# A graph-attention kernel in which the first turn waits for the one-hot: two banks of z, two banks of sums

## The chip, the cores and the metric

The kernel runs on one core of a Trainium2 chip. The metric is the device time of one execution in microseconds; the time of a version is the median over its runs.

## What is computed

One block of a graph network over 12,500 nodes with 128 features and 400,000 edges, which are sorted by their destination. After two norms of the nodes, a GATv2 attention with 8 heads of 16 features, a residual, a norm, and a two-layer GELU network follow:

```python
x_l = (x @ W_l).reshape(n, H, C)
x_r = (x @ W_r).reshape(n, H, C)
e = (ea @ W_e).reshape(-1, H, C)
m = jax.nn.leaky_relu(x_l[src] + x_r[dst] + e, NEG_SLOPE)
alpha = jnp.einsum('ehc,hc->eh', m, att)
amax = jax.ops.segment_max(alpha, dst, num_segments=n)
expa = jnp.exp(alpha - amax[dst])
denom = jax.ops.segment_sum(expa, dst, num_segments=n)
a = expa / (denom[dst] + 1e-16)
out = jax.ops.segment_sum(x_l[src] * a[:, :, None], dst, num_segments=n)
```

`loop` edges from each node to itself are part of it; the kernel deals with them where it finishes a group of nodes.

## The kernel before

A first part (about 190 us) norms the nodes and forms x_l and x_r. From then on the main loop goes through the edges in 782 **pairs** of 512 edges each. It is a software pipeline, one pair per **round**, and the order of its instructions is written out by hand: a table `stages` gives for each step the round in which it handles pair c, and in a round the steps are issued in the order of the table. A step of pair c in the steady part:

- `gather` (POOL, L1033): four indirect DMAs, 128 rows of x_l each, into a slot of a ring of 30 slots. The gathers of c reuse the slot of c-30 and wait until its sums are done.
- `place` (DVE, L1100, round c-1): the one-hot of the destinations, 96 rows of `ea`. The other 32 rows are the edges' attributes, loaded by DMA.
- `combine` (TensorE, round c): four transposes of the gathered rows into a bank of PSUM, the **turns** (L1127), and on top of them the **closing product** (L1132) of x_r's window and the edge weights with `ea`. The result is z = x_l[src] + x_r[dst] + e. Three banks of z take turns.
- `slope` (ACT, L1150, round c+1): zs = 0.2 z. `bend` (DVE, L1164, round c+1): m = max(z, zs).
- `score` (TensorE, L1185, round c+2, one round later for the first pair of a batch): the attention scores, 64 rows for a batch of eight pairs.
- Once per batch of eight pairs: scans for the lowest score of each segment (DVE, L1193 to L1214), the exponential (`weigh`, ACT, L1218), its transpose (`turn`, TensorE, L1225) and a copy of it beside the rows (`keep_turned`, ACT, L1235).
- `times` (DVE, L1246, round c+12): the gathered rows times their weights, in place in the ring.
- `own_nodes` (DVE, L1259, once per four pairs): the one-hot `own` of the destinations within a node window of 32, from `local` numbers that ACT copies into PSUM (L1295).
- `collect` (TensorE, L1277, round c+13): four products of `own` with the ring's rows, 32x144, the **sums** of the pair.
- `keep_sums` (ACT, L1289, round c+14): the copy `rec` of the sums out of PSUM, and L1308 the DMA that stores it.

In a round's order `keep_sums` and `put` stand first, then `collect`, `times`, `slope`, `combine`, `score`, `place`, `bend`. So in one round ACT begins with rec of c-1 and TensorE with sums of c. The work on finished groups of nodes (lines 1376 to 1632; names `f_...`, `acc`) and late parts of the first stage (lines 697 to 767; names `l_...`, `aux`) is woven into the rounds on fixed places.

PSUM has eight banks: before the change three of z, one of the scores, one of the turned weights `t`, one of the sums (three places of 144 columns, and two places of `local` beside them), `acc` and `aux`. Waits between engines are found by bank and by buffer: an instruction that writes or reads a bank waits for the last user of that bank on another engine. An engine waits by a semaphore that the other engine raises; `declare_no_dep` takes out a wait that another one covers, with its reason in the text.

Of the kernel before, what the change touches and what calls it, by code (L numbers as in the profile page):

```python
# [13 lines left out]
F32 = mybir.dt.float32  # L14
# [8 lines left out]
P = 128  # L23
# [14 lines left out]
QP = 4  # L38
# [10 lines left out]
W = 32  # L49
# [5 lines left out]
SX = P + 2 * H  # L55
# [876 lines left out]
def window_edges(  # L932
# [9 lines left out]
    nc = tc.nc  # L942
    SP = mybir.EngineType.SP
    KP = UP * KU
    EPR = UP * U
# [7 lines left out]
    pairs = [{} for _ in range(n_pr)]  # L953
    batches = []
    while not batches or batches[-1][-1] + 1 < n_pr:
        c = batches[-1][-1] + 1 if batches else 0
# [22 lines left out]
    with ExitStack() as es:  # L979
        once = es.enter_context(tc.tile_pool(name="e_once", bufs=1))  # L980
        load = es.enter_context(tc.tile_pool(name="e_load", bufs=2))
        work = es.enter_context(tc.tile_pool(name="e_work", bufs=3))
        ps1 = es.enter_context(tc.tile_pool(name="e_ps1", bufs=1, space=PSUM))
# [10 lines left out]
        ring = once.tile([P, RING, KP, SX], F32, name="ring")  # L994
# [102 lines left out]
        def place(c):  # L1097

            d = pairs[c]
            placed = nc.vector.tensor_scalar(  # L1100
                d["ea"][0:WN].rearrange("p (a b) -> p a b", b=OW),
                d["dl"][0:WN].rearrange("p (a b) -> p a b", b=OS)[:, :, 0:OW],
                wid[0:WN], None, op0=OP.is_equal,
            )
            if c % QP == 0:
                for ins in d["loads"]:
                    tc.add_manual_dep(
                        placed.ins, ins.name,
                        mybir.DependencyInfo(mybir.DependencyClass.Sync, mybir.DependencyReason.DATA),
                        reason="TensorE reads what was loaded beside the one-hot, and waits for VectorE alone",  # L1110
                    )

        scored = {}
        z_banks = [ps1.tile([P, EPR], F32, name=f"z{i}") for i in range(3)]
        z_used = []

        def z_bank():

            z_used.append(1)
            return z_banks[len(z_used) % 3]  # L1120

        def combine(c):

            d, e = pairs[c], sum(edges_of(c))
            z = z_bank()
            d["turns"] = [
                nc.tensor.matmul(  # L1127
                    z[:, j * P : (j + 1) * P], row_of(c, j)[:, 0:P], ident, start=(j == 0), stop=False, is_transpose=True
                ).ins
                for j in range(e // P)  # L1130
            ]
            d["closed"] = nc.tensor.matmul(z[:, :e], d["zw"], d["ea"][:, :e], start=False, stop=True).ins  # L1132
            d["z"] = z
            for ins in d["loads"]:
                tc.declare_no_dep(
                    d["closed"], ins, reason="VectorE waited for it ahead of the one-hot, which is read here too"
                )
            scored[c] = {i for i, p in enumerate(pairs[max(0, c - 9) : c], max(0, c - 9)) if "score" in p}
# [3 lines left out]
            for ins in pairs[c]["turns"]:  # L1142
                tc.declare_no_dep(reader.ins, ins, reason="TensorE made it ahead of the product that closes z")

        slopes = [work.tile([P, EPR], F32, name=f"zs{i}", bufs=1) for i in range(3)]

        def slope(c):
            d, e = pairs[c], sum(edges_of(c))
            d["zs"] = slopes[c % 3]
            sloped = nc.scalar.activation(d["zs"][:, :e], d["z"][:, :e], AF.Copy, scale=SLOPE)  # L1150
            only_last(sloped, c)
            if c >= 3:
                for ins in (pairs[c - 3]["bent"], pairs[c - 3]["sloped"]):
                    tc.declare_no_dep(
                        sloped.ins, ins, reason="TensorE waited for it ahead of z, which is read here"
                    )
            d["sloped"] = sloped.ins
# [105 lines left out]
                op=OP.is_equal,  # L1263
            )

        PLACES = 3
        sum_bank = ps1.tile([P, EPR], F32, name="sums")
        sum_at = [sum_bank[0:W, i * SX : (i + 1) * SX] for i in range(PLACES)]
        first = PLACES * SX
        local_at = [sum_bank[:, i : i + QP * KP] for i in (first, first + QP * KP)]  # L1270

        def collect(c):

# [11 lines left out]

        def keep_sums(c):
            d = pairs[c]
            d["rec"] = work.tile([W, SX], F32, name="rec", bufs=5)
            nc.scalar.copy(d["rec"], sum_at[c % PLACES])  # L1289
            if c >= n_pr - HASTE:  # L1290
                put(c)
            q, at = divmod(c + 2, QP)
            if at == 0 and q < len(fours):
                of_four[q]["local"] = local_at[q % 2]
                nc.scalar.copy(of_four[q]["local"], local_sb[:, q * QP * KP : (q + 1) * QP * KP])  # L1295
# [30 lines left out]
        sums = [None] * NL  # L1326
# [26 lines left out]
        def near_end(d):  # L1353
            return any(d is g for g in groups[-2:])
# [9 lines left out]
            return d[name][:, 0 : d["n"]]  # L1364

        def bank_of(d, name, ring="acc"):
            if near_end(d) and ring == "acc":
                ring = "z"
            d[name] = z_bank() if ring == "z" else ps1.tile([P, EPR], F32, name=ring)
            return d[name]  # L1370
# [425 lines left out]
        with tc.manual_schedule():  # L1796
            for r in range(-AHEAD, max(last_round, groups[-1]["round"] + 19)):
# [12 lines left out]
                for late, f in sum_stages:  # L1810
                    i, off = divmod(r - late, SUM_STEP)
# [10 lines left out]
                for late, f in late_stages:  # L1822
                    c = r - late
# [3 lines left out]
                if off == 0 and CLEARED <= t + CLEARED < NT and t >= 0:  # L1827
                    tc.declare_no_dep(
                        clear(t + CLEARED).ins, group="states",
                        reason="states stored so far lie below the tile, which the check of destinations asks",  # L1830
# [358 lines left out]
```

## Time and profile before

| what | value |
|---|---|
| median of 3 runs | 4851.8 us (4845.96 to 4852.41) |
| profiled execution | 4798.29 us |
| its span | 4796.5 us |
| mean granted TensorE clock | 0.875 |
| gathers, first to last start | 189.9 to 4660.0 us |
| DMA traffic | 536.78 MB, 112 GB/s over the span |

The profile is of one execution. A busy time is that of the engine's own instructions; "idle before" is the time in which an engine stood still ahead of an instruction, put down to what ended it. "issue" there means that the trace shows nothing that was waited for, and "remote" a word from an engine or queue that the trace does not name. PE is TensorE's matmuls and PEld its weight loads, which run beside them.

### The profile page before, as it was taken

What the parts mean: (1) busy time and instruction counts of PE and PEld (TensorE: products, weight loads), DVE (VectorE), ACT (ScalarE), POOL (GpSimd) and SP (SyncE); (2) the same over time, 40 slices, a digit from 0 to 9 for tenths busy, and PEclk for the clock granted to TensorE, in tenths of its full rate; (3) what the DMA queues carried; (4) which work ended last, traced back from release to release, by engine and by line L of the source; (5) the groups of instructions that cost most, each with busy time, mean ns of one, the idle gap of its engine ahead of it and who ended that gap; (6) DMA issues with size and microseconds to landing.
All of it is one profiled execution on the core that took longest, in us unless ns stands there. A gap on an engine that the chain in (4) does not pass through costs nothing.

```text
span 4796.5 us, 48948 instructions
## 1 busy us (share of the span) xinstructions
PE 3544.8 (74%) x14951; PEld 1790.8 (37%) x14952; DVE 2622.4 (55%) x4977; ACT 1502.6 (31%) x3825; POOL 2952.7 (62%) x3136
## 2 busy tenths in 40 slices
PE   3327777777777777777777877777778777777787
PEld 2203333333333333343333433333434333333344
DVE  5316555655655555556555555555555555555455
ACT  5302323322322323323333333333333333333222
POOL 6655666665666666666666666666666666666650
PEclk8658888888888989899898989898989898889898
DMA  6525555555543443444434334343344433434331
GB/s 185 164 75 151 141 145 144 148 146 147 142 132 93 112 110 102 104 112 105 106 93 106 100 98 102 98 101 101 91 99 108 100 100 98 102 86 103 100 96 31
DMA packets 425616, 536.78 MB, mean 112 GB/s; under 512 B 97241, under 2 KB 307210, under 8 KB 424794
## 3 DMA queue, kind: packets, MB, share of 16 engines
q1 hardware_dynamic: 282360, 266.19, 21.5%
q0 software_dynamic: 100000, 205.00, 16.5%
q10 hardware_dynamic: 42984, 62.37, 4.4%
q8 instruction: 121, 1.98, 0.2%
q14 instruction: 151, 1.24, 0.1%
HBM read 471.82 MB, written 61.42 MB: 111 GB/s over the span
## 4 chain that ended last, share of the span: by engine, by line
PE 38%; DVE 20%; another core or an unknown queue 15%; issue 12%; ACT 5%; DMA 2%; POOL 1%; ACTq 1%; SPq 0%; DVEq 0%; POOLq 0%
PE sums L1277 12%; PE z L1132 9%; PE s L1185 7%; PE z L1127 6%; DVE ea L1100 3%; DVE ring L1246 3%; DVE m L1164 3%; DVE s L1193 2%; DVE p L1207 2%; POOL ring L1033 1%; DVE p L1200 1%; ACT zs L1150 1%; ACT rec L1289 1%; PE acc L1612 1%
## 5 line engine op out<-in xcount | busy, mean ns | idle before, releaser
L1033 POOL DMA_INDIRECT ring<-xl_dram,idx_sb x3009 | 2839.8, 944 | 1637.4 <-issue 785.4
L1277 PE MATMUL sums<-ring,own 128*32 128x144 f32 x6250 | 1044.9, 317 | 979.2 <-ACT rec L1289 645.2
L1277 PEld LDWEIGHTS sums<-ring,own 128*32 128x32 f32 x6250 | 681.8, 119 | 1551.7 <-ACT rec L1289 801.2
L1164 DVE TENSOR_TENSOR m<-z,zs 128x512 f32<-128x512 f32 x782 | 532.8, 681 | 900.7 <-issue 538.8
L1132 PE MATMUL z<-ea,zw 128*128 128x512 f32 x1564 | 920.2, 674 | 10.9 <-issue 7.4
L1185 PE MATMUL s<-m,zneg 128*64 128x512 f32 x1564 | 851.2, 636 | 90.9 <-issue 71.4
L1150 ACT ACTIVATE zs<-z 128x512 f32<-128x512 f32 x782 | 464.8, 594 | 1171.5 <-PE z L1132 303.7
L1246 DVE TENSOR_TENSOR ring<-ring,t 128x512 f32<-128x512 f32 x782 | 527.8, 676 | 391.8 <-PE t L1225 179.4
L1127 PE MATMUL z<-ident,ring 128*128 128x128 f32 x3125 | 594.1, 320 | 25.2 <-DMA raw_dram<-raw 11.5
L1100 DVE TENSOR_SCALAR ea<-dl,wid 96x516 f32<-96x516 bf16 x782 | 577.7, 739 | 15.1 <-DMA zw<-xr_dram 15.1
L1289 ACT COPY rec<-sums 32x144 f32<-32x144 f32 x782 | 204.8, 262 | 1103.7 <-remote 332.0
L1127 PEld LDWEIGHTS z<-ident,ring 128*128 128x128 f32 x3125 | 379.8, 158 | 243.0 <-issue 218.1
L1185 PEld LDWEIGHTS s<-m,zneg 128*64 128x64 f32 x1564 | 165.7, 142 | 758.2 <-issue 635.0
L1193 DVE TENSOR_TENSOR_SCAN s<-g,s 64x512 f32<-64x512 bf16 x98 | 120.4, 1228 | 332.0 <-remote 100.6
L1132 PEld LDWEIGHTS z<-ea,zw 128*128 128x128 f32 x1564 | 279.3, 223 | 11.9 <-issue 8.0
L1259 DVE TENSOR_TENSOR own<-nodes,sums 128x512 f32<-128x512 f32 x195 | 132.6, 680 | 246.3 <-remote 190.0
L1218 ACT ACTIVATE p<-p 64x512 f32<-64x512 f32 x98 | 61.7, 630 | 330.0 <-DVE p L1207 128.8
L1235 ACT COPY ring<-t 128x256 f32<-128x256 f32 (+3 forms) x236 | 65.7, 344 | 253.7 <-DVE ring L1246 150.6
L326 POOL DMA_INDIRECT raw<-in_x,lead x92 | 88.9, 967 | 52.0 <-issue 26.6
L1207 DVE TENSOR_TENSOR_SCAN p<-g,s 64x512 f32<-64x512 bf16 x98 | 119.8, 1222 | 1.5
L1336 DVE TENSOR_REDUCE part<-ea_s 128x1 f32<-128x1024 f32 x98 | 118.3, 1207 | 0.0
L1218 ACT ACT_TABLE_LOAD x66 | 84.7, 1283 | 1.2
(244 smaller groups left out, 2248.5 us busy)
## 6 DMA issues: line engine op xcount, KB each, us to landing
dl<-dc_dram SPq DMA_DIRECT2D x196, 396.0 KB
ea_s<-in_ea_t ACTq DMA_DIRECT2D x98, 512.0 KB
ea<-in_ea_t SPq DMA_DIRECT2D x196, 256.0 KB
ring<-xl_dram,idx_sb POOLq DMA_INDIRECT x3009
state<-empty SPq DMA_DIRECT2D x98, 144.0 KB
f_st<-state SPq DMA_DIRECT2D x48, 288.0 KB
state<-rec ACTq DMA_DIRECT2D x782, 13.5 KB
zw<-xr_dram SPq DMA_DIRECT2D x196, 48.0 KB
```

The source lines that it names most:

```text
L1033: rows = nc.gpsimd.indirect_dma_start(out=slot(c)[:, j, 0:P], out_offset=None, in_=xl_dram, in_offset=bass.IndirectOffsetOnAxis(ap=index(c ...
L1100: placed = nc.vector.tensor_scalar(d["ea"][0:WN].rearrange("p (a b) -> p a b", b=OW), d["dl"][0:WN].rearrange("p (a b) -> p a b", b=OS)[:, ...
L1127: nc.tensor.matmul(z[:, j * P : (j + 1) * P], row_of(c, j)[:, 0:P], ident, start=(j == 0), stop=False, is_transpose=True).ins
L1132: d["closed"] = nc.tensor.matmul(z[:, :e], d["zw"], d["ea"][:, :e], start=False, stop=True).ins
L1150: sloped = nc.scalar.activation(d["zs"][:, :e], d["z"][:, :e], AF.Copy, scale=SLOPE)
L1164: bent = nc.vector.tensor_tensor(d["m"][:, :e], d["z"][:, :e], d["zs"][:, :e], op=OP.max)
L1185: d["score"] = nc.tensor.matmul(of_batch[b]["s"][0:HB, :e], zneg[:, k : k + HB], d["m"][:, :e], start=(i == 0), stop=(c == batches[b][-1]) ...
L1193: nc.vector.tensor_tensor_scan(d["s"][HB:P], d["g"][:, 0:EPR], d["s"][0:HB], BIG, op0=OP.add, op1=OP.min)
L1207: nc.vector.tensor_tensor_scan(d["p"][0:HB, back], d["g"][:, 1 : EPR + 1][:, back], d["s"][HB:P][:, back], BIG, op0=OP.add, op1=OP.min)
L1246: product = nc.vector.tensor_tensor(rows, rows, weights[:, 0:k].to_broadcast([P, k, C, H]), op=OP.mult)
L1277: nc.tensor.matmul(sum_at[c % PLACES], own[:, c % QP * KP + j, :], slot(c)[:, j, :], start=(j == js[0]), stop=(j == js[-1]),).ins
L1289: nc.scalar.copy(d["rec"], sum_at[c % PLACES])
```

## The change

It has four parts that hang together.

- There are two banks of z in place of three, and two slope buffers in place of three. The first turn of pair c waits for place of c (a dependency added by hand), where the closing product did so before. TensorE raises its semaphore once for the five products, at the closing product.
- The bank that is set free holds sums: two banks with three places each. Pair c goes to bank c mod 2. Each bank also holds one place of `local`, those of group q in bank q mod 2.
- `rec` has six buffers in place of five.
- The last groups of nodes, which took banks of z, take `aux` for two of their products and `acc` for one.

```diff
@@ def place(c):
-            placed = nc.vector.tensor_scalar(
+            d["placed"] = placed = nc.vector.tensor_scalar(
...
-        z_banks = [ps1.tile([P, EPR], F32, name=f"z{i}") for i in range(3)]
+        z_banks = [ps1.tile([P, EPR], F32, name=f"z{i}") for i in range(2)]
...
-            return z_banks[len(z_used) % 3]
+            return z_banks[len(z_used) % 2]
@@ def combine(c):
+            tc.add_manual_dep(
+                nc.get_inst_by_name(d["turns"][0].name), d["placed"].ins.name,
+                mybir.DependencyInfo(mybir.DependencyClass.Sync, mybir.DependencyReason.DATA),
+                reason="the product that closes z reads the one-hot and waits for nothing itself",
+            )
@@ slope(c)
-        slopes = [work.tile([P, EPR], F32, name=f"zs{i}", bufs=1) for i in range(3)]
+        slopes = [work.tile([P, EPR], F32, name=f"zs{i}", bufs=1) for i in range(2)]
...
-            if c >= 3:
-                for ins in (pairs[c - 3]["bent"], pairs[c - 3]["sloped"]):
+            if c >= 2:
+                for ins in (pairs[c - 2]["bent"], pairs[c - 2]["sloped"]):
...
-        PLACES = 3
-        sum_bank = ps1.tile([P, EPR], F32, name="sums")
-        sum_at = [sum_bank[0:W, i * SX : (i + 1) * SX] for i in range(PLACES)]
-        first = PLACES * SX
-        local_at = [sum_bank[:, i : i + QP * KP] for i in (first, first + QP * KP)]
+        PLACES = 6
+        IN_BANK = 3
+        sum_banks = [ps1.tile([P, EPR], F32, name=f"sums{i}") for i in range(PLACES // IN_BANK)]
+        sum_at = [
+            sum_banks[i % 2][0:W, i // 2 * SX : (i // 2 + 1) * SX] for i in range(PLACES)
+        ]
+        local_at = [bank[:, IN_BANK * SX : IN_BANK * SX + QP * KP] for bank in sum_banks]
@@ def keep_sums(c):
-            d["rec"] = work.tile([W, SX], F32, name="rec", bufs=5)
+            d["rec"] = work.tile([W, SX], F32, name="rec", bufs=6)
@@ def bank_of(d, name, ring="acc"):
-            if near_end(d) and ring == "acc":
+            if near_end(d) and name in ("z", "sc"):
+                ring = "aux"
+            elif near_end(d) and ring == "acc" and name != "wp":
                 ring = "z"
```

The order of the instructions on each engine stays as it was; the waits move. On TensorE, in the middle of the main loop (sums of pairs 361 and 362 with combine of 374 and the score of 372 between them), before:

```order
L1277 MATMUL sums_1662<-ring_1650,own_14405 32x144 [waits DVE_49,Activation_49]
L1277 MATMUL sums_1662<-ring_1650,own_14405 32x144 x3
L1127 MATMUL z0_1653<-ident_80,ring_1650 128x128 [waits DMASW0_49]
L1127 MATMUL z0_1653<-ident_80,ring_1650 128x128 [waits DMASW1_49]
L1127 MATMUL z0_1653<-ident_80,ring_1650 128x128 [waits DMASW2_49]
L1127 MATMUL z0_1653<-ident_80,ring_1650 128x128 [waits DMASW3_49]
L1132 MATMUL z0_1653<-ea_14265,zw1_1646 128x512 [waits DVE_49]
L1185 MATMUL s_14361<-m0_1659,zneg_87 64x512 [waits DVE_49]
L1277 MATMUL sums_1662<-ring_1650,own_14405 32x144 [waits DVE_49,Activation_49]
L1277 MATMUL sums_1662<-ring_1650,own_14405 32x144 x3
```

and with the change, at the same place:

```order
L1284 MATMUL sums1_1661<-ring_1650,own_14404 32x144 [waits DVE_49,Activation_49]
L1284 MATMUL sums1_1661<-ring_1650,own_14404 32x144 x3
L1127 MATMUL z1_1654<-ident_80,ring_1650 128x128 [waits DMASW0_49,DVE_49]
L1127 MATMUL z1_1654<-ident_80,ring_1650 128x128 [waits DMASW1_49]
L1127 MATMUL z1_1654<-ident_80,ring_1650 128x128 [waits DMASW2_49]
L1127 MATMUL z1_1654<-ident_80,ring_1650 128x128 [waits DMASW3_49]
L1137 MATMUL z1_1654<-ea_14264,zw1_1646 128x512
L1190 MATMUL s_14360<-m0_1657,zneg_87 64x512
L1284 MATMUL sums0_1660<-ring_1650,own_14404 32x144 [waits DVE_49,Activation_49]
L1284 MATMUL sums0_1660<-ring_1650,own_14404 32x144 x3
```

The closing product and the score have lost their waits for DVE, and the first turn has one, for bend of two pairs before (and with it for place of its own pair, which stands just ahead on DVE). The sums wait for ACT as before, but now by their own bank, for the copy two pairs back.

On ACT, the copies of the sums of pairs 359 and 360 (`state` is the DMA that stores an older copy), before:

```order
L1289 COPY rec_14434<-sums_1662 32x144 [waits DMAHW3_49,DVE_49,Activation_49]
L1308 DMA state_69<-rec_14347 24x576 [waits DMAHW1_49]
L1150 ACTIVATE zs0_1656<-z1_1654 128x512 [waits PE_49]
L1417 ACTIVATE f_zs_14451<-acc_14412,el_1644 128x512 [waits PE_49]
L1289 COPY rec_14465<-sums_1662 32x144 [waits DMAHW4_49,PE_49]
```

and with the change:

```order
L1296 COPY rec_14433<-sums1_1661 32x144 [waits DMAHW2_49,PE_49]
L1315 DMA state_69<-rec_14346 24x576 [waits DMAHW3_49,DMAHW1_49]
L1155 ACTIVATE zs0_1655<-z1_1654 128x512 [waits PE_49]
L1426 ACTIVATE f_zs_14450<-acc_14411,el_1644 128x512 [waits PE_49]
L1296 COPY rec_14464<-sums0_1660 32x144 [waits DVE_49,PE_49,Activation_49]
```

The wait for `own` (DVE) sits on the copy of the first pair of a group of four here, where it was on the last pair of the group before it: group 90 is even, and its `local` numbers are in the other bank than the sums of pair 359. For the odd groups they are in the same bank, and those rows stand as before.

More of the change, by code (lines that the diff above doesn't have):

```diff
@@ L1143, in only_last @@
                 tc.declare_no_dep(reader.ins, ins, reason="TensorE made it ahead of the product that closes z")
-        slopes = [work.tile([P, EPR], F32, name=f"zs{i}", bufs=1) for i in range(3)]
+        slopes = [work.tile([P, EPR], F32, name=f"zs{i}", bufs=1) for i in range(2)]
         def slope(c):
             d, e = pairs[c], sum(edges_of(c))
-            d["zs"] = slopes[c % 3]
+            d["zs"] = slopes[c % 2]
             sloped = nc.scalar.activation(d["zs"][:, :e], d["z"][:, :e], AF.Copy, scale=SLOPE)
             only_last(sloped, c)
-            if c >= 3:
-                for ins in (pairs[c - 3]["bent"], pairs[c - 3]["sloped"]):
+            if c >= 2:
+                for ins in (pairs[c - 2]["bent"], pairs[c - 2]["sloped"]):
                     tc.declare_no_dep(
```

## The prediction

> **What bounds the kernel now.** I read the page's engine totals first, then its groups of instructions, the waits of TensorE, the waits of POOL, and last the timeline of ten rounds (2376 to 2430 us). From the page:
>
> ```profile
> span 4796.5 us, 48948 instructions
> PE 3544.8 (74%) x14951; PEld 1790.8 (37%) x14952; DVE 2622.4 (55%) x4977; ACT 1502.6 (31%) x3825; POOL 2952.7 (62%) x3136
> ...
> L1033 POOL DMA_INDIRECT ring<-xl_dram,idx_sb x3009 | 2839.8, 944 | 1637.4 <-issue 785.4
> L1277 PE MATMUL sums<-ring,own 128*32 128x144 f32 x6250 | 1044.9, 317 | 979.2 <-ACT rec L1289 645.2
> ```
>
> PE is the busiest engine, and 979.2 us of its idle time stand ahead of one step, the sums. What ends it, by TensorE's waits:
>
> ```profile
> PE sums L1277 <- ACT rec L1289: 645.2, 192, 9.9
> PE sums L1277 <- issue: 137.7, 84, 7.3
> PE sums L1277 <- ACT sums L1295: 79.5, 46, 6.0
> ```
>
> So ACT's copy out of the one bank of sums holds TensorE in most of it: sums of c wait for rec of c-1, which ACT makes at the head of the same round. The timeline shows why so small a copy is late. These rows are of pairs 355 (the first sums) to 364 (the last); the four pairs without idle ahead of their sums are left out. A row has start, duration, engine, line, and in brackets the idle time before it with what ended it.
>
> ```profile
> 2376.72 1.17 PE L1277 MATMUL sums<-ring,own 128*32 128x144 f32 x8 [0.74 <-ACT sums L1295]
> ...
> 2377.81 0.66 PE L1127 MATMUL z<-ident,ring 128*128 128x128 f32 x4
> ...
> 2378.30 1.02 PE L1132 MATMUL z<-ea,zw 128*128 128x512 f32 x2
> ...
> 2380.31 0.67 DVE L1259 TENSOR_TENSOR own<-nodes,sums 128x512 f32<-128x512 f32 x1
> ...
> 2381.06 0.27 ACT L1289 COPY rec<-sums 32x144 f32<-32x144 f32 x1 [0.47 <-ACT xr L710]
> ...
> 2381.38 1.17 PE L1277 MATMUL sums<-ring,own 128*32 128x144 f32 x8 [1.05 <-ACT rec L1289]
> ...
> 2387.59 0.60 ACT L1150 ACTIVATE zs<-z 128x512 f32<-128x512 f32 x1 [6.27 <-issue]
> ...
> 2388.22 0.69 DVE L1164 TENSOR_TENSOR m<-z,zs 128x512 f32<-128x512 f32 x1 [5.98 <-issue]
> ...
> 2388.39 1.17 PE L1277 MATMUL sums<-ring,own 128*32 128x144 f32 x8 [2.81 <-issue]
> ...
> 2389.49 0.97 PE L1127 MATMUL z<-ident,ring 128*128 128x128 f32 x4
> ...
> 2392.84 0.67 DVE L1246 TENSOR_TENSOR ring<-ring,t 128x512 f32<-128x512 f32 x1
> ...
> 2394.10 0.67 DVE L1164 TENSOR_TENSOR m<-z,zs 128x512 f32<-128x512 f32 x1
> ...
> 2395.69 2.12 PE L1277 MATMUL sums<-ring,own 128*32 128x144 f32 x8 [3.52 <-ACT rec L1289]
> ...
> 2397.75 1.12 PE L1127 MATMUL z<-ident,ring 128*128 128x128 f32 x4
> ```
>
> ```profile
> 2409.10 0.27 ACT L1289 COPY rec<-sums 32x144 f32<-32x144 f32 x1 [0.58 <-issue]
> ...
> 2409.30 0.66 DVE L1246 TENSOR_TENSOR ring<-ring,t 128x512 f32<-128x512 f32 x1
> ...
> 2412.36 1.17 PE L1277 MATMUL sums<-ring,own 128*32 128x144 f32 x8
> ...
> 2413.30 0.69 DVE L1164 TENSOR_TENSOR m<-z,zs 128x512 f32<-128x512 f32 x1 [2.68 <-ACT zs L1150]
> ...
> 2416.96 1.13 DVE L748 SCALAR_TENSOR_TENSOR l_xl<-aux,l_r,bl_r 128x128 f32<-128x128 f32 x4 [2.96 <-remote]
> 2417.05 0.27 ACT L1289 COPY rec<-sums 32x144 f32<-32x144 f32 x1 [3.78 <-remote]
> ...
> 2417.28 0.94 POOL L1033 DMA_INDIRECT ring<-xl_dram,idx_sb  x1 [2.06 <-remote]
> 2417.37 1.17 PE L1277 MATMUL sums<-ring,own 128*32 128x144 f32 x8 [1.39 <-ACT rec L1289]
> ...
> 2418.46 0.42 PEld L1127 LDWEIGHTS z<-ident,ring 128*128 128x128 f32 x4 [0.23 <-issue]
> ...
> 2427.99 0.69 DVE L1259 TENSOR_TENSOR own<-nodes,sums 128x512 f32<-128x512 f32 x1 [6.20 <-remote]
> ...
> 2429.07 1.17 PE L1277 MATMUL sums<-ring,own 128*32 128x144 f32 x8 [3.55 <-issue]
> ```
>
> Two things are to be seen. The sums of pair 361 begin at 2412.36 and are done at 2413.53, yet ACT copies them only at 2417.05, and DVE and POOL, which wait for PE too, go on within 0.3 us of it. Likewise z of pair 368 is closed at 2378.30 + 1.02 = 2379.32 and ACT begins its slope at 2387.59, 8.27 us later. TensorE's word reaches the others late and in bursts, and POOL's pause of 2.06 us ends in the same burst. Any wait that a whole round trip through another engine feeds thus costs microseconds; a wait for something one round older mostly costs none.
>
> **The change part by part.** *The sums.* Pairs alternate between two banks, so sums of c wait for rec of c-2; three places in a bank add nothing beyond that, since the wait goes by bank. In each of the six idle times I ask what stands next, with the other engines where they were:
>
> - 355 (0.74 us): the local destinations of an odd group of four lie in bank 1, where sums of 4q-1 go as well, so this wait stays. Gain 0.
> - 356 (1.05): it needs the one-hot `own`, ended 2380.98, which still waits for the sums of 355 in an odd group. The rec that ends at 2381.33 is followed by its sums 0.05 us later, so I put 0.05 on each telling: start 2381.03, gain 0.35.
> - 357 (2.81): the sums could go nearly at once, but the turns behind them then meet the new wait, for bend of 368, ended 2388.91. They started at 2389.49: gain 0.53.
> - 358 (3.52): times ends at 2392.84 + 0.67 = 2393.51, the sums start at 2395.69: gain 2.13. The turns behind them, at 2397.75, move to 2395.6, after bend of 369 (2394.77).
> - 362 (1.39): rec of 360 was done at 2409.37, times at 2409.96, bend of 373 at 2413.99, long before the turns at 2418.46: gain 1.39, whole.
> - 364 (3.55): `own` of the next odd group ends at 2428.68: gain 0.34.
>
> Together 4.74 of 13.06 us, 36%. What is late next is thus `own`, then times behind the scans, then bend. Of the 979.2 us this is 355 us.
>
> *The turns' wait.* Turn 0 of c now waits for place of c and, with two banks of z, for bend of c-2, which DVE makes right behind that place. Queued behind it on TensorE are the closing product, score, and the next round's sums; ACT's slope and DVE's bend wait for those. In the ten rounds it limits only pair 357's gain, and that is already counted. The closed product and the score wait for nothing any more. Place comes about 0.5 us sooner due than before, since four turns (0.66 us) stood ahead of its reader; bend behind it on DVE is the later bound anyway, so nothing is added.
>
> *The waits as instructions.* The first turn now has two things to wait for, the gather and DVE, and the second stands as an instruction of its own in TensorE's queue: the changed program has 752 more of these (1361 for 609). The trace's price for one:
>
> ```profile
> L1277 PEldq EVENT_SEMAPHORE  x489: 51/51/51, 368.5 to 4754.9; - x163
> ```
>
> 752 x 51 ns = 38 us if none lies in the shadow of the running matmuls, 0 if all do. I take the middle, 19.
>
> *The telling.* 4 x 782 turns no longer tell each for itself; TensorE's tellings fall from 4525 to 2578. No row gives the price of one. The gain lies between 0 and the 137.7 us of idle ahead of the sums that nothing shown has ended; I take 0 in the sum, since the sample's largest such idle (2.81 and 3.55 us) has causes that stay, and keep half of it, 69, for the range. The Trainium skill ("TensorE: Matmul & The Clock Gate", "The cost: per-tile semaphore tail") has increments serialize at 26.3 ns each; by it the turns' 3128 would be worth at most an estimated 82 us, and the sum 82 us lower. The lateness of 3.5 and 8.3 us above is far more than such a tail, and no run here shows yet which part belongs to it.
>
> *The rest.* Slopes go from three to two: the buffer's old reader, bend of c-2, is what turn 0 has waited for, so nothing. Six rec buffers for five loosen a wait for DMAs that ends no large idle time: 0. The last groups' banks touch only the tail, behind the last gather: within 5 us either way, and I take 0.
>
> Sum: 355 - 19 = 336 us, 7.0% of the profiled execution's 4798.3 us, which becomes 4462. The median of the runs is 4851.8; the same 336 us off it give 4516, so **4515 us**. A floor: POOL's gathers are busy 2839.8 us, and 785.4 us between them wait for nothing shown; with the 190 us ahead of the first and the 136 us behind the last,
>
> ```profile
> L1033 POOL DMA_INDIRECT ring<-xl_dram,idx_sb x3009: 938/944/2197, 189.9 to 4660.0; - x189
> ```
>
> that is 3951 us, so POOL does not stop this gain.
>
> **The rivals.**
>
> *Late words grow later.* The bursts come when POOL stands still: POOL's idle time ended by a word from elsewhere or from TensorE is
>
> ```profile
> POOL ring L1033 <- remote: 420.9, 189, 2.9
> POOL ring L1033 <- PE sums L1277: 190.6, 47, 35.7
> POOL ring L1033 <- PE z L1132: 92.8, 75, 2.9
> POOL ring L1033 <- PE z L1127: 45.2, 38, 2.7
> ```
>
> 749 us. Taking 336 us out of the rounds leaves 413 of that, so pauses, and with them the words, come rarer. If half of the gain goes back, 168 us remain: 4685. If all of it does, nothing changes: 4850. For it speaks the common instant at 2417; against it, that waits a round older have more slack than that.
>
> *Two banks of z close a loop (slower).* Closed of c, told after a delay D, slope 0.60, bend 0.69, then turns of c+2 (their product starts 0.49 after them, 2378.30 against 2377.81) make two rounds of 1.02 + D + 0.60 + 0.69 + 0.1 + 0.49 = 2.9 + D. A round takes (4660.0 - 189.9) / 782 = 5.72 us now. So the loop decides once D averages over 11.4 - 2.9 = 8.5 us. With D at 9 in half of the rounds, they last 0.25 us longer: about 100 us, 4950. One D of 8.27 is seen above (pair 368), and there the bend was done only 0.58 us ahead of the turns two pairs on. Against it: the bends of 369 and 373 had 2.98 and 4.47 us to spare.
>
> *The clock.* The granted clock by stretches of the span (the column after the five engines):
>
> ```profile
> 1420.00:2420.00 1000.00, 779.71 (x3335) 391.60 (x3335) 553.96 (x1005) 320.60 (x768) 638.23 (x678) 0.90 0.41 106
> ...
> 2389.70:2399.90 10.20, 6.68 (x20) 3.38 (x18) 7.53 (x13) 4.02 (x14) 5.82 (x7) 0.50 0.18 48
> ```
>
> Right behind the idle 2.81 us PE ran at 0.50, and stayed there over the next idle 3.52. At 0.90 on the mean, a fifth of the steady 4200 us lies at half clock, 840 us; PE is busy 65% of such a stretch (6.68 of 10.20), and full clock would save half of that, 275 us. If shorter idle times lift half of it, the time is 4515 - 135 = 4380; all of it, 4240. The Trainium skill's page named above ("Why this matters for your kernels") says that idle gaps over about 3 us bring the half clock back; the row at 0.50 fits, and by that rule this rival is what follows if those gaps go. Against it: four of the six idle times above keep most of their length.
>
> **How the numbers follow.** The forecast has 0.49; half of it given back 0.18 (4685); the clock's share on top 0.11 (4380); no change 0.08 (4850); the loop of two z banks 0.14 (4950). About 0.2%, 10 us, is what a measurement here can tell from no change: faster 0.49 + 0.18 + 0.11 = 0.78, same 0.08, slower 0.14. The range leaves out the slower case and the lower half of the clock's: 4290 (4380 less the 19 for the waits and the 69 for the tellings, rounded) to 4860.
>
> **What would show it.** Right: idle ahead of the sums falls from 979 to about 620 us, with rec's share down most and `own` or times as the names that are left; turns show a few tens of us of waits for bend; PE's busy time stays near 3545 and POOL's pauses shrink by some 300 us. The loop would show as hundreds of us of idle ahead of the turns. Late words would show as idle ahead of slope and rec that grows. Wrong altogether: idle ahead of the sums unchanged, or a granted clock that moves by more than 0.03.

## The result, and the profile after

The changed kernel takes 4800.27 us (median of 4 runs, 4788.99 to 4804.03) against 4848.88 us of the kernel before beside it: a ratio of 0.9904, with a 95% interval of 0.9876 to 0.9932. It is faster by 49 us, a seventh of the 336 us that were forecast; it lies inside the stated range of 4290 to 4860 us only because that range reaches up to no change. A second set of runs (e13 below) gave 0.9928 (0.9906 to 0.9951).

The two profiles must be read with one thing in mind: the profiled execution of the kernel before took 4798.29 us, 47 us under the lowest of its other runs, and that of the changed kernel 4804.03 us, which is like its other runs. The time of the first lies among those of the kernel before on the chip of e5 and e6 below (4773.13 to 4801.28), so it may come from another chip than they do, which nothing here settles. What follows shows where the idle time went; the 49 us themselves can't be read off this pair.

From the page of the changed kernel, in its groups the busy time, the mean, and the idle time before with what ended most of it:

```profile
span 4802.2 us, 49742 instructions
...
L1033 POOL DMA_INDIRECT ring<-xl_dram,idx_sb x3009 | 2847.3, 946 | 1645.2 <-issue 803.9
L1284 PE MATMUL sums<-ring,own 128*32 128x144 f32 x6250 | 1040.8, 315 | 897.9 <-DVE own L1264 238.1
...
L1190 PE MATMUL s<-m,zneg 128*64 128x512 f32 x1564 | 849.7, 636 | 5.4 <-DVE p L1219 2.4
...
L1127 PE MATMUL z<-ident,ring 128*128 128x128 f32 x3125 | 596.6, 320 | 188.4 <-issue 99.8
```

and the rows of the kernel before that answer to the last two:

```profile
L1185 PE MATMUL s<-m,zneg 128*64 128x512 f32 x1564 | 851.2, 636 | 90.9 <-issue 71.4
...
L1127 PE MATMUL z<-ident,ring 128*128 128x128 f32 x3125 | 594.1, 320 | 25.2 <-DMA raw_dram<-raw 11.5
```

Idle time ahead of sums, score and turns together was 979.2 + 90.9 + 25.2 = 1095.3 us and is 897.9 + 5.4 + 188.4 = 1091.7 us. In these two executions of nearly the same length it changed its place and its names. Beside e1 below, which keeps the wait for rec and took 4850.18 us in its profiled execution, the changed kernel has 48 us less of it (there it is 1009.6 + 99.3 + 30.4 = 1139.3 us), about what its execution is shorter. TensorE's waits in the changed kernel:

```profile
PE sums L1284 <- DVE own L1264: 238.1, 61, 9.4
PE sums L1284 <- ACT p L1223: 195.0, 40, 12.8
PE sums L1284 <- DVE ring L1251: 161.9, 32, 10.0
...
PE z L1127 <- issue: 99.8, 40, 17.7
...
PE z L1127 <- DVE m L1169: 63.0, 20, 15.3
...
PE sums L1284 <- ACT rec L1296: 18.2, 8, 9.4
```

and the rows of the kernel before for the same names:

```profile
PE sums L1277 <- DVE ring L1246: 12.0, 7, 2.3
...
PE z L1127 <- DVE m L1164: 9.0, 1, 9.0
...
PE sums L1277 <- ACT p L1218: 4.1, 3, 2.3
...
PE sums L1277 <- DVE own L1259: 2.6, 3, 1.1
```

The wait that the change is about fell from 645.2 to 18.2 us, as meant. The one-hot `own`, the exponential `p`, `times` (written `ring`) and bend (`m`, ahead of the turns), which ended nearly nothing before, stand in its place. POOL did not gain room either: 2839.8 busy and 1637.4 idle before, 2847.3 and 1645.2 now. Counting the breaks of over 1 us between one gather and the next, there are 314 in each trace, 802 and 807 us long in all (36 and 37 us of it one long break at the start). These breaks are late words too. The first gather of a pair waits for the sums of 30 pairs back. Following the pairs through the changed kernel's trace from 420 to 4400 us, those sums were done before POOL stood still in 237 of 290 breaks, by a median of 3.3 us, and POOL still went on only 2.5 us (median) after it had stopped. Before the change it was 223 of 292.

The timeline of the changed kernel shows how the new names come about:

```profile
2393.52 1.07 PE L1190 MATMUL s<-m,zneg 128*64 128x512 f32 x2
...
2397.57 0.69 DVE L1169 TENSOR_TENSOR m<-z,zs 128x512 f32<-128x512 f32 x1 [6.11 <-issue]
...
2399.40 0.94 POOL L1033 DMA_INDIRECT ring<-xl_dram,idx_sb  x1 [0.30 <-issue]
2399.99 1.23 DVE L1198 TENSOR_TENSOR_SCAN s<-g,s 64x512 f32<-64x512 bf16 x1 [1.73 <-PE z L1137]
...
2403.19 0.96 POOL L1033 DMA_INDIRECT ring<-xl_dram,idx_sb  x1 [2.85 <-remote]
...
2403.89 0.67 DVE L1251 TENSOR_TENSOR ring<-ring,t 128x512 f32<-128x512 f32 x1
...
2404.71 2.10 PE L1284 MATMUL sums<-ring,own 128*32 128x144 f32 x8 [4.88 <-DVE ring L1251]
...
2421.99 1.17 PE L1284 MATMUL sums<-ring,own 128*32 128x144 f32 x8
...
2423.68 0.94 POOL L1033 DMA_INDIRECT ring<-xl_dram,idx_sb  x1 [0.30 <-issue]
...
2426.52 0.27 ACT L1296 COPY rec<-sums 32x144 f32<-32x144 f32 x1 [3.82 <-remote]
...
2426.76 0.94 POOL L1033 DMA_INDIRECT ring<-xl_dram,idx_sb  x1 [2.14 <-PE sums L1284]
```

Below, the sums of one pair end at 2423.16; POOL's last gather of a run ends at 2424.62, and only 1.9 us after that do ACT (2426.52) and POOL (2426.76), which both wait for these sums, go on, together. Above, the scores that DVE's scan needs are done at 2394.59 and the scan begins at 2399.99, 5.4 us later. DVE stood idle for 6.11 us ahead of bend first, and for another 1.73 us ahead of the scan, while POOL was still at its gathers; `times` stands behind the scan's chain, and the sums wait 4.88 us for `times` instead of for rec. So some words do pass during a run, late, and others come in common bursts behind its end.

How late a word is can be worked out over the whole loop (420 to 4400 us): from the end of TensorE's instruction, or from when the waiting engine fell idle if that was later, to the start of the instruction that waits for it. The profiler models the ends of matmuls, so it is the comparison between runs that counts. For DVE's scan the mean is 1.73 us before and 2.83 us after, up to 9.76 us; it is 0.04 us in e3, e4, e7, e8 and e18 below. For ACT's copy rec it is 1.62 and 2.00 us, against 0.25 in e4. DVE's bend behind ACT's slope, a word of ACT, has 0.03 us in all of these runs. So it is TensorE's words that are late. Of those over 1 us late in the changed kernel, 113 of 185 copies and 28 of 47 scans began in a break of POOL or within 0.3 us behind it, but only 37 of 186 slopes did, no more than by chance, since the breaks with these 0.3 us take 20% of the time.

### The profile page after: what moved, and what is told of

Its sections match the earlier page's. It is cut to its first block, busy times and chain, and to the rows that moved or that the text cites. A ratio compares the mean times of both kernels' runs of the same rounds, so it can differ in the third digit from the quotient of the medians.

```text
span 4802.2 us, 49742 instructions
## 1 busy us (share of the span) xinstructions
PE 3551.5 (74%) x14951; PEld 1796.5 (37%) x14952; DVE 2622.6 (55%) x4977; ACT 1481.5 (31%) x3825; POOL 2960.4 (62%) x3136
## 5 line engine op out<-in xcount | busy, mean ns | idle before, releaser
L1033 POOL DMA_INDIRECT ring<-xl_dram,idx_sb x3009 | 2847.3, 946 | 1645.2 <-issue 803.9
L1284 PE MATMUL sums<-ring,own 128*32 128x144 f32 x6250 | 1040.8, 315 | 897.9 <-DVE own L1264 238.1
L1127 PE MATMUL z<-ident,ring 128*128 128x128 f32 x3125 | 596.6, 320 | 188.4 <-issue 99.8
```

The lines of the kernel that those rows point to most:

```text
L1033: rows = nc.gpsimd.indirect_dma_start(out=slot(c)[:, j, 0:P], out_offset=None, in_=xl_dram, in_offset=bass.IndirectOffsetOnAxis(ap=index(c ...
L1127: nc.tensor.matmul(z[:, j * P : (j + 1) * P], row_of(c, j)[:, 0:P], ident, start=(j == 0), stop=False, is_transpose=True).ins
L1284: nc.tensor.matmul(sum_at[c % PLACES], own[:, c % QP * KP + j, :], slot(c)[:, j, :], start=(j == js[0]), stop=(j == js[-1]),).ins
```

## The experiments

Five chips were used for them. The kernel before ran beside each set, and its time tells the chips apart: 4842, 4794 and 4850 us on three of them, and 3989 us on two, which are called prompt chips below. All ratios are to the kernel before on the same chip.

My theory after the result (F in the expectations): on chips like that of the forecast POOL's gathers hold up TensorE's words to the other engines until POOL stops, so the rounds go at the pace of POOL's runs and stops, whatever TensorE waits for. The count above bears out the first half; the second, that only a stop lets them through, holds for some three in five of the late copies and scans and not for the slopes. Its rivals: the removed wait was followed by other waits of equal length that have nothing to do with POOL (W), or the gathered rows themselves come too late (P).

**Half the change alone (e1, e2; kernel before 4842).** e1 is the kernel before with only this:

```diff
-            placed = nc.vector.tensor_scalar(
+            d["placed"] = placed = nc.vector.tensor_scalar(
...
+            tc.add_manual_dep(
+                nc.get_inst_by_name(d["turns"][0].name), d["placed"].ins.name,
...
```

> The kernel before, with one edit: the first turn waits for the one-hot of its own pair, so TensorE tells once for the four turns and the closing product. Three banks of z and one bank of sums stay. Theory F (frozen words: TensorE's words come through only when POOL stands still between gathers, and each such pause costs about 2.5 us): fewer words at each pause make the rest come sooner, so this edit alone gives at least half of the 48 us, 4805 to 4825. Theory W (new holders: the wait for rec was merely followed by other waits of the same round, and the words have nothing to do with it): the gain of the change is that of the second bank of sums, and this kernel stays at 4849 within 10 us.

4850.35 us, 1.0015 (0.9998 to 1.0033): no gain. TensorE's tellings are 2393 here against 4525, so telling once is worth nothing that can be measured, and my expectation from F, half of the gain, fell; that from W was met. The Trainium skill ("TensorE: Matmul & The Clock Gate", "The cost: per-tile semaphore tail") counts 26.3 ns for each increment in the tail of a group of tiles; no run here shows that, where by its figure some 2100 fewer would come to an estimated 56 us.

e2 is the changed kernel with one bank of sums:

```diff
-        PLACES = 6
-        IN_BANK = 3
...
+        PLACES = 3
+        sum_bank = ps1.tile([P, EPR], F32, name="sums")
+        sum_at = [sum_bank[0:W, i * SX : (i + 1) * SX] for i in range(PLACES)]
...
```

> The changed kernel with its sums in one bank again (three places), everything else as changed: two banks of z, told once. Theory F: told once stays, the wait for rec one round back returns, but either wait ends with the same burst of words; 4800 to 4830. Theory W: without the second bank the gain is gone, and two banks of z cost something: 4850 to 4900. By the forecast's own sum for the bank (355 us of idle) it would have to stand far above the changed kernel, at 5100; I expect that to fall.

4846.03 us, 1.0000 (0.9982 to 1.0019). Here, too, F's 4800 to 4830 fell, and W's 4850 to 4900 was missed by 4 us. Two banks of z and one telling cost nothing and bring nothing; what is left for the second bank of sums is the whole gain, 0.7 to 1.0%. The changed kernel itself was not run on this chip. The wait for rec is back in the trace of e2, with the turns' wait beside it:

```profile
L1282 PE MATMUL sums<-ring,own 128*32 128x144 f32 x6250 | 1044.1, 317 | 995.8 <-ACT rec L1294 643.8
...
L1190 PE MATMUL s<-m,zneg 128*64 128x512 f32 x1564 | 860.2, 643 | 7.2 <-issue 4.7
...
L1127 PE MATMUL z<-ident,ring 128*128 128x128 f32 x3125 | 593.0, 320 | 125.9 <-issue 85.2
```

995.8 + 7.2 + 125.9 = 1128.9 us of idle time on the three steps, 37 us more than in the changed kernel's trace: of some 630 us of waits for rec that the bank takes out, about 37 stay out.

**Without gathers (e3, e4; same chip).** Plain transfers from SyncE fill the ring, in the kernel before and in the changed one. The rows are then not those of the edges' sources.

```diff
+            if c >= 0:
+                at = c * EPR % (xl_dram.shape[0] - EPR)
+                rows = nc.sync.dma_start(
+                    slot(c)[:, :, 0:P], xl_dram[at : at + EPR].rearrange("(j p) f -> p j f", p=P)
+                )
...
+                return
```

> The kernel before, with POOL's indirect gathers of the main loop replaced by one plain transfer of 512 rows in order for each pair, issued by SyncE, the same bytes into the same slots with the same wait for the sums of the slot's last pair. It leaves out the choice of rows by source. Theory F: TensorE's words are no longer held up, the idle time ahead of the sums falls below 350 us, slopes follow their product within 1 us, and the time falls by 400 us or more, to 4450 or less. Theory W: the chain of waits is the same and the time stays within 100 us of 4849.

> The changed kernel with the same plain transfers in place of the gathers. Theory F: about as fast as the kernel before with plain transfers, within 60 us on either side, since prompt words leave little for a second bank of sums to win. Theory W: the change's gain stands as with gathers, near 4800.

3772.22 us (0.7789; 0.7766 to 0.7812) and 3653.09 us (0.7541; 0.7515 to 0.7566). W falls: it had the time within 100 us of 4849, and 22% of the time hangs on POOL's gathers. Between the two the change brings 119 us, 3.2%, more than with gathers; F had less than 60. The sums in e3 and in e4:

```profile
L1285 PE MATMUL sums<-ring,own 128*32 128x144 f32 x6250 | 944.4, 296 | 330.9 <-ACT rec L1297 304.9
```

```profile
L1292 PE MATMUL sums<-ring,own 128*32 128x144 f32 x6250 | 929.3, 293 | 251.7 <-ACT p L1231 130.5
```

With prompt words rec's wait was 304.9 us, and 79 us of idle time ahead of the sums go for good. The rest of the 119 is mostly TensorE's own busy time, 3285.4 us in e3 and 3239.2 in e4, at granted clocks of 0.948 and 0.962.

**Gathers that nobody reads (e5, e6; kernel before 4794).** As e3 and e4, but POOL still issues its four gathers a pair, into spare tiles:

```diff
                     rows = nc.gpsimd.indirect_dma_start(
-                        out=slot(c)[:, j, 0:P],
+                        out=spare[(c * KP + j) % 8],
...
```

> The kernel before with plain transfers filling the ring, and POOL still issuing its four gathers a pair, with the same wait for the sums of 30 pairs back, into eight spare tiles that nobody reads. Theory F (POOL's gathers hold up TensorE's words to all engines): the words are late again, and the time goes back to 4700 to 4900 although no result depends on a gather. Theory P (POOL's pace: the rows themselves came too late, 1.25 us a gather and a pause of 2.5 us for each burst): rows come from the plain transfers in time, and it runs at 3772 to 4000.

> The changed kernel with plain transfers in the ring and the same spare gathers on POOL. Theory F: 4650 to 4850, and 20 to 80 us under the kernel before with spare gathers. Theory P: 3653 to 4000, and about 119 us under it.

4801.47 us (1.0028; 1.0010 to 1.0046) and 4745.28 us (0.9902; 0.9882 to 0.9922). Nothing reads these gathers, the rows come from the plain transfers, and both kernels are back near their full times, as F had it; between them the change brings 56 us. That decides between F and P: the gathers act on TensorE though no data goes from them to it. Nor does TensorE wait for other transfers that they could crowd: of its waits in e6 the profile puts only one down to a DMA, 24.5 us. In e6 the idle time ahead of the sums is back, too:

```profile
L1039 POOL DMA_INDIRECT spare<-xl_dram,idx_sb x3009 | 2840.5, 944 | 1587.1 <-issue 802.5
L1289 PE MATMUL sums<-ring,own 128*32 128x144 f32 x6250 | 1034.4, 314 | 817.7 <-issue 315.4
```

**Half the gathers, and other work on POOL (e7, e8; same chip).** e7 takes two of four tiles by a plain transfer; half of the rows are then not the sources'. e8 has plain rows, and on POOL fills in place of the spare gathers.

```diff
+                slot(c)[:, 0:2, 0:P], xl_dram[at : at + 2 * P].rearrange("(j p) f -> p j f", p=P)
...
+                    if j < 2:
+                        continue
                     rows = nc.gpsimd.indirect_dma_start(
```

```diff
-                    rows = nc.gpsimd.indirect_dma_start(
...
+                    rows = nc.gpsimd.iota(
+                        spare[(c * KP + j) % 2], pattern=[[1, EPR]], base=0, channel_multiplier=0,
...
```

> The changed kernel with two of the four gathers of a pair replaced by a plain transfer of 256 rows in order. Half of the rows are then not those of the sources. Theory F: POOL issues half as long for each burst, so words are held up half as long; about midway between 4800 and 3653, 4000 to 4400. Theory P: POOL's own time falls to half, 2000 us and pauses, so it no longer sets the pace: 3653 to 3800.

> The changed kernel with plain transfers in the ring, and POOL busy with four fills of a spare tile (an iota of 128x512, which should last about as long as a gather, 0.7 to 1.0 us) in place of the gathers, with the same wait for the sums. If any busy POOL holds up TensorE's words: 4500 or more. If it is the issue of gathers: within 100 us of 3653.

3731.09 us (0.7786; 0.7769 to 0.7804) and 3658.66 us (0.7626; 0.7609 to 0.7643). Half the gathers cost only 72 us over none (e8), where F had a middle value, 4000 to 4400; the time lies where P had it, but P fell with e5 and e6. The hold does not grow in step with the gathers: the scan's words are as prompt here, 0.04 us, as without any. In e8 words are prompt; of one pair's sums, done at 2001.00, ACT hears by 2001.04 and POOL by 2001.13:

```profile
1999.83 1.17 PE L1287 MATMUL sums<-ring,own 128*32 128x144 f32 x8
...
2001.04 0.27 ACT L1299 COPY rec<-sums 32x144 f32<-32x144 f32 x1 [3.48 <-PE sums L1287]
...
2001.13 2.10 POOL L1039 IOTA spare<- 128x512 f32 x4 [3.43 <-PE sums L1287]
```

But a fill lasted only 0.575 us on the mean, so POOL was busy with them 1577 us, near the 1419 us of e7's gathers. e8 shows that plain rows and a POOL that is half busy hold up nothing; it does not show that a POOL as busy as with all gathers, but with other work, would not.

**Fills between the gathers, and an earlier one-hot (e9 to e12; kernel before 3989).** These fell on a prompt chip. The edits to the changed kernel: behind each gather an iota of 128x1 (e9) or 128x128 (e10, shown); both places of `local` in bank 0 (e11); and in e12 ACT also copies them two rounds earlier.

```diff
+                    nc.gpsimd.iota(spare, pattern=[[1, 128]], base=0, channel_multiplier=0, allow_small_or_imprecise_dtypes=True)
```

```diff
-        local_at = [bank[:, IN_BANK * SX : IN_BANK * SX + QP * KP] for bank in sum_banks]
+        first = IN_BANK * SX
+        local_at = [sum_banks[0][:, i : i + QP * KP] for i in (first, first + QP * KP)]
...
-            q, at = divmod(c + 2, QP)
+            q, at = divmod(c + 4, QP)
```

> The changed kernel with one short POOL instruction (an iota of 128x1, 0.13 us in the kernel before) behind each gather. It spaces the 3009 gathers by 0.13 us more, 391 us in all. If the words pass in any short break between gathers, POOL's pauses (314 in the main loop, 2.5 us each) shrink by more than that: 4500 to 4780. If a burst's backlog has to drain as a whole, and the drain goes on beside a short fill only for the fill's time, the pauses shorten by about what the fills add: 4780 to 4900. If the fills do nothing for the words: 4800 + 391 = 5190.

> The same with a fill of 0.26 us (an iota of 128x128) behind each gather, 794 us in all: 4500 to 4780 if words pass in the breaks, 4800 to 5000 if the drain merely moves into the fills, up to 5590 if they do nothing.

> The changed kernel with both places of the local destinations in bank 0, so that the one-hot of an odd group no longer waits for the sums of the round before it, of bank 1, but for those one round older, as in the even groups. In the changed kernel 238 us of idle time ahead of the sums end with that one-hot. If POOL's bursts set the pace, little of it shows: 4770 to 4800. If the wait itself does: 4680 or less.

> As with the local destinations in bank 0, and ACT copies them two rounds earlier, behind the sums of pair 4q-4 in place of 4q-2, so that the one-hot needs no recent word of TensorE. If POOL's bursts set the pace: 4740 to 4800. If the wait for the one-hot does: 4620 or less, 238 us with what hangs on it.

4065.60 us (1.0190; 1.0175 to 1.0206), 4399.19 (1.1028; 1.1011 to 1.1045), 3981.57 (0.9980; 0.9971 to 0.9989) and 3981.01 (0.9980; 0.9971 to 0.9989). The expectations were written for a chip that holds words up and say nothing here. In e11 and e12 no gap of POOL between gathers is over 0.32 us, and in e9 and e10 the fills lengthen its row of gathers.

**Again, on a chip that holds words up (e13 to e15; kernel before 4850).** The changed kernel, e12's and e9's.

> The changed kernel once more, beside the kernel before on one chip. Two of the three chips so far hold TensorE's words up behind POOL's gathers (4842 and 4794 for the kernel before), the third does not (3989, no pause of POOL over 0.8 us, and TensorE waits for gathered rows). On a chip that holds them up: 40 to 60 us faster, as the first result. On one that does not: POOL's gathers are the bound there (2841 us busy and 808 between them), the waits that the change moves end nothing, and it is within 15 us of the kernel before, near the 0.998 of the two kernels with the local destinations moved.

> The changed kernel with the local destinations in bank 0 and copied two rounds earlier, once more. On a chip that holds words up: the one-hot's 238 us of idle time go, but POOL's bursts stay, so 0 to 60 us under the changed kernel; 150 us or more under it would mean that the waits set the pace there and not the bursts. On one that does not: equal to the changed kernel within 8 us.

> The changed kernel with a short POOL instruction behind each gather, once more. On a chip that does not hold words up it cost 77 us on 3989, so not its 391 us but what does not fit beside the 0.3 us between gathers. On a chip that does: if the words pass in short breaks, 4100 to 4500; if only a stop of POOL lets them through, 4800 to 5000.

4814.92 us (0.9928; 0.9906 to 0.9951), 4826.24 (0.9947; 0.9927 to 0.9967) and 4806.94 (0.9922; 0.9893 to 0.9950). The changed kernel is 35 us faster than the kernel before, a little under what I expected; e14 is not under it, where F had it 0 to 60 us under. In e14 the one-hot itself hardly waits any more: 2.8 us of idle time stand ahead of `own` on DVE, against 233.5 in e13. Yet TensorE's wait that ends with it falls only from 247.0 to 200.0 us, so DVE reaches `own` late by what stands ahead of it there, and the time does not follow. The sums and the turns, and the wait for `own`, of e13, then of e14:

```profile
L1284 PE MATMUL sums<-ring,own 128*32 128x144 f32 x6250 | 1039.0, 315 | 887.4 <-DVE own L1264 247.0
...
L1127 PE MATMUL z<-ident,ring 128*128 128x128 f32 x3125 | 596.3, 320 | 198.0 <-issue 108.9
...
PE sums L1284 <- DVE own L1264: 247.0, 63, 9.0
```

```profile
L1285 PE MATMUL sums<-ring,own 128*32 128x144 f32 x6250 | 1038.3, 314 | 804.9 <-ACT p L1223 201.9
...
L1127 PE MATMUL z<-ident,ring 128*128 128x128 f32 x3125 | 596.5, 319 | 242.8 <-issue 139.2
...
PE sums L1285 <- DVE own L1264: 200.0, 46, 10.9
```

Ahead of the sums 82 us are gone, 45 of them stand ahead of the turns, and the run is no shorter. The fills of e15 keep POOL busy for 457 us more,

```profile
L1042 POOL IOTA spare<- 128x1 f32 x3009 | 457.4, 152 | 30.2 <-remote 9.8
```

and cost nothing: they lie in the gaps between gathers and in what had been breaks (those over 1 us are 694 us in all here and 813 us in e13). Nor do they free the words; the scan's are 3.18 us late on the mean.

**Longer fills, and the change on a prompt chip (e16 to e18; kernel before 3989).** e16 is e10's kernel again, e17 has the same fill behind each second gather only (an `if j % 2:` ahead of it), and e18 is the changed kernel beside them.

> The changed kernel with a POOL fill of 0.26 us behind each gather, once more. Where words are prompt it ran at 4399, so the gathers start 1.35 us apart (4399 less about 330 ahead and behind, by 3009). On a chip that holds words up: if the hold comes from the density of gathers and 1.35 us is loose enough, words pass and it runs at 4400 to 4550, under the changed kernel; if a stop of POOL is still needed, the pauses come on top: 4850 to 5300.

> The same fill behind each second gather, so the gathers start about 1.28 us apart in the mean, 3850 us in all and 4180 with what lies ahead and behind. On a chip that holds words up: 4200 to 4500 if that is loose enough, 4750 to 4900 if pauses are still needed. On one that does not: 4130 to 4250.

> The changed kernel, on the chip of the two fills. On a chip that holds words up 4750 to 4815 and 0.988 to 0.995 of the kernel before; on one that does not, within 15 us of the kernel before, at about 3981.

4399.22 us (1.1030; 1.1014 to 1.1047), 4183.69 (1.0489; 1.0473 to 1.0505) and 3983.07 (0.9986; 0.9977 to 0.9995). The chip was a prompt one again. e18 gives the change's worth there, within the 15 us expected: 0.14%, 6 us. Its trace has no break between gathers over 0.32 us, and TensorE waits for rows; its page, and the waits of POOL and TensorE:

```profile
L1033 POOL DMA_INDIRECT ring<-xl_dram,idx_sb x3009 | 2842.4, 945 | 921.0 <-issue 806.2
```

```profile
POOL ring L1033 <- issue: 806.2, 2645, 0.3
```

```profile
PE z L1127 <- DMA ring<-xl_dram,idx_sb: 321.1, 259, 5.4
```

POOL's 2842.4 + 921.0 us between the first gather and the last are the bound here, and a shorter wait of TensorE for ACT or DVE does not shorten them. e17 and e16 agree: with 1504 and 3009 fills of about 0.26 us the time grows by 201 and 416 us over e18.

## Why the prediction was right and wrong

- *Faster:* right, by 0.7 to 1.0% on the chips like that of the forecast, by the way named (the second bank of sums).
- *What bounds the kernel.* That rec's late copy ended most of TensorE's idle time was read rightly: that wait went from 645.2 to 18.2 us. That it bounded the kernel was wrong. The rows with common instants (2416.96, 2417.05, 2417.28) were on the table, and the burst was named; each wait was still priced by itself.
- *The step that failed: "with the other engines where they were".* The 36% that may be gained held every other time fixed, `own`, `times` and bend among them. But on these chips ACT, DVE and POOL all hear TensorE late. Where one wait is moved a round back, others that hang on TensorE's words take its place (`own` from 2.6 to 238.1 us, `p` from 4.1 to 195.0, `times` from 12.0 to 161.9, bend from 9.0 to 63.0). Of 355 us that the sum had, the comparison with e2 finds 37 (idle time) to 46 (medians, of two sets of runs). e14 is another case of it: with the wait of `own` itself nearly gone, TensorE's wait for it kept four fifths of its length, and nothing was gained.
- *The floor.* I set POOL's at 3951 us and said that POOL does not stop this gain. I had left its breaks out, as waits for others. They are waits, but mostly for words already due (237 of 290 breaks), and moving TensorE's waits does not bring those sooner: 2839.8 + 1637.4 us before, 2847.3 + 1645.2 after, the same number of breaks. 3951 is about what the prompt chips show (3983), where POOL does stop all but 6 us of it.
- *The rivals.* "Late words grow later" came nearest and had 0.18, with 0.08 for all of the gain given back; neither of its prices was met: six sevenths were. The words did grow later. The copies for which ACT stood idle were 1.4 to 1.6 us late in the four runs with one bank of sums (the kernel before, e1, e2, e5) and 1.8 to 2.0 in the three with two (the changed kernel, e6, e13); the slopes 1.1 to 1.3 and 1.4. The reason given, rarer pauses of POOL, does not show: there are 314 in both traces. The loop of two z banks shows as 163 us more idle ahead of the turns, but e2 puts its cost at zero. The clock did not move (0.875 and 0.867).
- *Small terms.* One telling for five is worth nothing (e1), and by the trace 1947 tellings went, not the 3128 of all turns. The 752 more wait instructions, two slopes and six rec buffers can't be seen in any run apart; e2 holds them all, and is at 1.0000.
- *The signs to look for* served. Two held, though they could not tell the size: rec's share fell most, with `own` and `times` among the names left, and PE's busy time stayed (3551.5 us). Idle ahead of the sums at 620 (897.9), a few tens of us ahead of the turns (188.4) and 300 us less break on POOL (none) all failed, and said the same thing.

What stays open: why the five chips differ; why the slopes' late words come at other times than the rest; and, on a chip that holds words up, how sparse the gathers must be to let the words pass. Half of them is sparse enough (e7). Fills that space all of them to 1.28 and 1.35 us were meant to tell more, and ran on prompt chips. Nor do the runs say which part of a gather does it, POOL's issue or the transfers that follow. e8 points to the gathers and not to a busy POOL, but its POOL was half idle. No kernel tried that computes the result beats the changed one by more than its interval on either kind of chip.

## What to carry to other kernels

When several engines resume within a few tenths of a microsecond of each other, look for what they have in common before pricing any one engine's wait: a share worked out with the others held still was seven to ten times too high here, and the first experiment is to take the common suspect away whole (here POOL's gathers, which cost 22%). Idle time that an engine spends between bursts may be part of its pace, and a floor made of its busy time alone is too low. A time from one chip is a time of that chip; run the kernel before beside each change.

## What the runs showed of the hardware

TensorE's words to ACT, DVE and POOL were held up beside POOL's indirect gathers at full density (four of 0.944 us in each pair, 0.30 us apart), on three chips of five: by 1.73 to 2.83 us on the mean for DVE's scan in the two main traces, up to 9.76 us, against 0.04 us with plain transfers (e3, e4, e8). Gathers that nothing reads do the same (2.16 and 2.05 us in e5 and e6), half as many do not (0.04 us in e7). Words of ACT and DVE are prompt beside it: TensorE goes on 0.05 us behind ACT's copy (2381.33 to 2381.38 in the kernel before), DVE's bend 0.03 us behind ACT's slope. On the two other chips the kernel before took 3989 us in place of some 4840, the scan's words are 0.04 us late (e18), and the changed one's trace there shows no break of POOL over 0.32 us.
